# A two-layer graph network on one core: the prelude's order, the decoding of neighbour lists, and where the last lists are made

## The chip, the cores and the metric

The kernel runs on 1 core of a Trainium2 chip. The time is device microseconds of one execution; the number compared is the median over repeated executions. TensorE is called PE (PEld its weight loads), VectorE DVE, ScalarE ACT, GpSimd POOL, SyncE SP. Each engine works through its own instructions in the order of the program; DMA transfers are issued from the queues of SP, ACT and POOL.

## What is computed

x has 3327 rows of 512, adj is a symmetric 0/1 matrix of 3327 x 3327 with a full diagonal and some 9 ones in a row. Two layers, each with a residual and a normalisation:

```python
# layer 0: four heads of 128
feats = einsum('nf,hfo->hno', X, W)
e_s, e_n = feats . a_self, feats . a_neigh               # one number per head and node
logits = leaky_relu(e_s[:, :, None] + e_n[:, None, :], 0.2) + NEG_INF * (1 - A)
out = relu(concat_h(softmax(logits) @ feats) + b)
x = layernorm(x + out)
# layer 1
attn_a = sigmoid([adj @ x, x] @ Wa.T + ba);  attn_b = sigmoid([adj @ x, x] @ Wb.T + bb)
h = x @ W_sa;  scores = (h @ a_sa_left)[:, None] + (h @ a_sa_right)[None, :]
e = where(adj != 0, exp(-leaky_relu(scores, 0.01)), 0);  x_a = e / (sum(e) + 1e-5) @ h
x_b = adj @ (x @ W_gcnb) + b_gcnb
x = layernorm(x + sigmoid(attn_a * x_a + attn_b * x_b))
```

## The kernel before

**Sparse work.** The kernel reads adj once, makes a list of neighbours for each node, and then gathers rows by those lists. The 3328 padded nodes are 26 tiles of 128: a first group of 12 tiles and a second of 14 (`NG`). Within a group nodes are sorted by degree, so that tile j needs only `CAPS[j]` neighbour slots (14 down to 5, and 14 down to 4). Only if a check at the end finds something that the lists don't cover does `dense_pass` run; it doesn't with these inputs.

**Prelude (L199 to L634).** adj and x come in seven chunks of 512 columns (the last has 256). SP's queue holds the loads in this order: W0, x0, x1, then for each chunk 13 pairs of adjacency tiles (L221, `AT` = 12 buffers) and x of the chunk after next (L212, 3 buffers). ACT's queue loads the two rows a_neigh and a_self, W_sa and the two halves of a_sa. For each tile `features` (L362) makes 8 accumulations x W0 on PE (260 columns per half: 256 features and 4 score columns), ACT copies them into a row of 520, and POOL writes it to `table0` in DRAM (L379). The score columns of W0 are made first: DVE and POOL multiply W0 with a broadcast row, DVE reduces (L302, L309). The vectors of W_sa, needed for the scores of layer 1, are made by POOL products and DVE reductions (L339, L340).

**Lists.** For a chunk, `make_codes` (L389) multiplies the adjacency tiles with powers of two on PE, so that each block of 16 nodes becomes one number: a code of 16 bits and the block's number in its low bits. `turn_codes` transposes them. `top_codes` (L421) takes the 24 largest codes of each node (`S` = 24) with MAX8 and MATCH_REPLACE8 on 224 columns. `decode` (L427) splits off the highest bit of each code `LEVELS` = 4 times, giving 4 x 24 candidates, and `pick` (L445) takes the 24 largest of these 96 and turns them into node numbers, in `st0` or `st1`, and degrees. All of it is DVE work. `rank_a` and `rank_b` (L474, L484) rank a group's nodes by degree, with two matmuls and a scan. The first group's lists are sorted through DRAM: 12 indirect writes on POOL (L145), one load back (L529), then 12 gathers of x (`own_x`, L557); the tasks are handed out three at a time between projections (`later`). The second group's lists are sorted on PE, two of 14 steps in each of seven rounds of layer 0 (`sort1`, L534).

**The loop of the prelude (L608 to L634).** Three projections, then for each chunk: codes, one projection, turn, top, decode, pick, four projections. Ranks of the first group are ready in chunk 3's round, those of the second after chunk 6. Only then is layer 0 reached.

**Layer 0 (L863 to L922).** `gather` (L644) issues one indirect DMA on POOL for each slot of a tile (L667), into 7 buffers of up to 6 slots (`GB`, `U`), three tiles ahead. All gathers read `table0`, and so stand behind all its row writes. For a tile, `weigh_a` and `weigh_b` make the softmax weights on DVE; `attend` (L800) scales two of three gathered rows on DVE and one on ACT, and PE adds them up with an identity matrix (L820). Then come the residual (L898), the statistics, and the products with the score vectors `v1` (`columns1` to `columns3`, L834 to L848); groups of finished tiles are normalised and written to `table1`. The order of tiles (`order0`) begins with the first group's tiles 11, 10, 0, 1, 2 and so on: slots 6, 7, 16, 13, 12, 11. Tile 0 of each group has extra slots (`stair`), placed with `to_nodes` and `to_rows` on PE; `climb` prepares them.

**Layer 1 (L927 to L1122)** gathers from `table1` in the same manner and ends with the output's indirect writes.

Of the kernel before, what the change touches and what calls it, by code (L numbers as in the profile page):

```python
# [14 lines left out]
P = 128  # L15
# [14 lines left out]
LW = 32  # L30
# [4 lines left out]
AT = 12  # L35
# [44 lines left out]
def sparse_pass(  # L80
# [50 lines left out]
    B = len(STAIRS)  # L131
    C0 = CAPS[0]
# [6 lines left out]
    table1 = dram.tile([NP, ROW], F32, name="table1")  # L139
    own1 = dram.tile([NG[1] * P, 2, ROW], F32, name="own1")  # L140
    lists0 = dram.tile([NG[0] * P, LW], I32, name="lists0")

# [20 lines left out]
    ovf = const.tile([P, NT, 3], F32, name="ovf")  # L163
# [44 lines left out]
    def load_x(i):  # L208
        if i < len(chunks):
            cw = min(CH, NP - chunks[i])  # L210
            xc = xcs[i] = pj.tile([P, KT, CH], F32, tag="xc", name=f"xc{i}", bufs=3)
            nc.sync.dma_start(xc[:, :, :cw], xB[i] if cw == CH else xL)  # L212

    halves = halves_of(NT)
    loaded = {}

    def load_adj(i):
        cw = min(CH, NP - chunks[i])
        for q, (a, b) in enumerate(pairs_of(NT)):
# [7 lines left out]
    wsa0 = pj.tile([P, KT, F], F32, name="wsa0")  # L227
    nc.scalar.dma_start(wsa0, W_sa.rearrange("(k p) o -> p k o", p=P))
    asa_rows = []
    for s in range(2):  # L230
        a_row = pj.tile([P, F], F32, name=f"asa_row{s}")
        nc.scalar.dma_start(a_row, row_bcast(a_sa, F, s * F))
        asa_rows.append(a_row)
    load_x(1)
    for i in range(len(chunks)):
        load_adj(i)
        load_x(i + 2)
# [36 lines left out]
    all1 = p0.tile([P, ND * NM], F32, name="all1")  # L274
    nc.gpsimd.memset(all1, 1.0)

    st0 = p0.tile([P, NG[0], LW], I32, name="st0")
# [3 lines left out]
    count = dict(channel_multiplier=1, allow_small_or_imprecise_dtypes=True)  # L281
    W1 = S + 2 + H
# [11 lines left out]
    def st(t):  # L294
        return (st0[:, t, :], st0[:, t, S + 2 : S + 2 + H].bitcast(F32)) if t < NG[0] else (
            st1[:, t - NG[0], :], st1[:, t - NG[0], S + 2 : S + 2 + H]
        )

    for s in range(2):
        for hh in range(2):  # L300
            prod = pj.tile([P, KT, 2, FO], F32, tag="prod", name=f"prod{s}_{hh}", bufs=4)
            (nc.vector, nc.gpsimd)[s].tensor_mul(  # L302
                prod,
                w0[:, :, hh, 0 : 2 * FO].rearrange("p k (h o) -> p k h o", h=2),
                a_rows[s][:, hh * 2 * FO : (hh + 1) * 2 * FO]
                .rearrange("p (k h o) -> p k h o", k=1, h=2)
                .to_broadcast([P, KT, 2, FO]),
            )
            nc.vector.tensor_reduce(w0[:, :, s, 2 * FO + 2 * hh : 2 * FO + 2 * hh + 2], prod, AX.X, ALU.add)  # L309
# [12 lines left out]
    with nc.allow_non_contiguous_dma(reason="four vectors of 512, onto partitions"):  # L322
        for i, w in enumerate((Wa, Wb)):
            for s in range(2):
                src = w[0:1, s * F : (s + 1) * F].rearrange("o (k p) -> p (o k)", p=P)
                nc.gpsimd.dma_start(v1[:, :, 3 * s + 1 + i], src)
    nc.gpsimd.dma_start(bias0, row_bcast(b0, F))
# [5 lines left out]

    for s in range(2):
        for k in range(KT):
            prod = pj.tile([P, F], F32, tag="prod1", name=f"sprod{s}_{k}", bufs=2)
            nc.gpsimd.tensor_mul(prod, wsa0[:, k], asa_rows[s])  # L339
            nc.vector.tensor_reduce(v1[:, k, 3 - 3 * s : 4 - 3 * s], prod, AX.X, ALU.add)  # L340

    nc.gpsimd.tensor_add(v1[:, :, 4:6], v1[:, :, 4:6], v1[:, :, 1:3])
    nc.gpsimd.tensor_add(v1[:, :, 6], v1[:, :, 0], v1[:, :, 3])

    in_step = p0.tile([P, P], F32, name="in_step")
    nc.gpsimd.memset(in_step, 1.0)
    nc.gpsimd.memset(no_step, 0.0)
    for b, n in enumerate(STAIRS):
        o = sum(STAIRS[:b])
        nc.gpsimd.tensor_copy(to_row[:, o : o + n], ident[:, :n])  # L350
        nc.gpsimd.affine_select(
            in_step[:, o : o + n], in_step[:, o : o + n], pattern=[[0, n]], compare_op=ALU.is_equal, fill=0.0,
            base=-b, channel_multiplier=1,
        )
        nc.gpsimd.affine_select(
            no_step[:, b : b + 1], no_step[:, b : b + 1], pattern=[[0, 1]], compare_op=ALU.is_ge, fill=-BIG,
            base=n - 1, channel_multiplier=-1,
        )
# [3 lines left out]
    def features(t):  # L362
# [4 lines left out]
        pf = psf.tile([P, 2, 512], F32, tag="pf", name=f"pf{t}")  # L367
        for k, hh in ((k, hh) for hh in range(2) for k in range(KT)):
            nc.tensor.matmul(  # L369
                pf[:, hh, :HC], xc[:, k, o : o + P], w0[:, k, hh, :], start=(k == 0), stop=(k == KT - 1)  # L370
            )
        row = pj.tile([P, ROW], F32, tag="row", name=f"row{t}", bufs=4)
# [5 lines left out]
        nc.scalar.copy(st(t)[1], pf[:, 1, F // 2 : HC])  # L378
        nc.gpsimd.dma_start(table0[t * P : (t + 1) * P, :], row)  # L379

    widths = [32 * ((len(ms) + 3) // 4) for ms in halves]
    vs, pvs, ents, cands, codes_left = {}, {}, {}, {}, {}
# [6 lines left out]
    def make_codes(i):  # L389

        own0, nt = span(i)[:2]
        v = vs[i] = p0.tile([P, 2, CH], F32, tag="v", name=f"v{i}", bufs=2)
        for half, ms in enumerate(halves):
# [1181 lines left out]
```

## Time and profile before

| | |
|---|---|
| 14 runs | median 959.32 us (953.42 to 963.75) |
| profiled execution | 965.76 us, its span 963.8 us |
| prelude up to the first tile's weights | 0 to 219.5 us |
| layer 0 | 219.5 to some 556 us |
| layer 1 | some 556 to 963.8 us |
| busy: PE, DVE, POOL, ACT | 798.4, 742.3, 615.7, 278.7 us |
| granted TensorE clock, mean | 0.898 |
| DMA: bytes, mean rate | 221.41 MB, 230 GB/s |

Busy time of POOL counts the issue of a gather at about 1.0 us; the next one starts 0.3 us later even when nothing holds it, so POOL can be saturated at three quarters busy. A busy time of PE counts matmuls that overlap. The rate of DMA counts both the prelude's loads and everything that is written.

### The profile page before, as it was taken

How to read it: one execution, taken by the hardware profiler on the slowest of the kernel's cores; microseconds unless marked ns; L12 is line 12 of the kernel's file. 1: busy time of each engine (PE TensorE's matmuls, PEld its weight loads, DVE VectorE, ACT ScalarE, POOL GpSimd, SP SyncE). 2: the span in 40 equal slices, each digit the busy share in tenths (PEclk: the TensorE clock that was granted, in tenths of full speed). 3: DMA queues.
4: the chain of work that ended last, by engine and by line, in shares of the span. 5: the costliest groups of instructions: out<-in, count | busy, mean ns of one | idle time of the engine just before them, and what ended most of it. 6: DMA issues, size and time to landing. Idle time of an engine off the chain costs nothing.

```text
span 963.8 us, 10097 instructions
## 1 busy us (share of the span) xinstructions
PE 798.4 (83%) x2516; PEld 419.7 (44%) x2516; DVE 742.3 (77%) x2175; ACT 278.7 (29%) x820; POOL 615.7 (64%) x654
## 2 busy tenths in 40 slices
PE   4398997328999887979969839998999989899893
PEld 3176775114545444434434414444434434344341
DVE  4277677786988588687757838799989989989873
ACT  1022121002435244335333403213222232232241
POOL 6611134775677767677777467777777777777511
PEclk9699998557899899899988958999989999999998
DMA  9799899998678777887777266767676676666401
GB/s 319 285 356 401 339 339 372 379 400 287 171 207 248 208 243 222 270 271 232 229 224 232 105 177 190 197 187 186 192 192 197 184 192 190 187 187 182 139 22 47
DMA packets 71986, 221.41 MB, mean 230 GB/s; under 512 B 12912, under 2 KB 16960, under 8 KB 71024
## 3 DMA queue, kind: packets, MB, share of 16 engines
q0 software_dynamic: 46560, 153.64, 53.9%
q1 hardware_dynamic: 22704, 64.94, 17.7%
q10 hardware_dynamic: 2656, 2.10, 0.7%
q8 instruction: 23, 0.38, 0.2%
q14 instruction: 43, 0.35, 0.1%
HBM read 199.78 MB, written 28.32 MB: 237 GB/s over the span
## 4 chain that ended last, share of the span: by engine, by line
PE 42%; DVE 20%; DMA 15%; POOL 12%; issue 7%; ACT 3%; DVEq 0%; POOLq 0%; ACTq 0%
PE acc L820 17%; DMA g<-table,srt 10%; PE pf L369 9%; POOL g L667 9%; DVE sw L1025 7%; PE po L1065 5%; PE acc L1046 4%; DMA at<-in_adjB 4%; DVE g L1027 3%; PE pcol L844 2%; DMA a_row<-in_a_self 1%; POOL sprod L339 1%; PE sorted L548 1%; ACT za L1110 1%; DVE za L1093 1%
## 5 line engine op out<-in xcount | busy, mean ns | idle before, releaser
L667 POOL DMA_INDIRECT g<-table,srt x464 | 482.4, 1040 | 160.6 <-issue 119.5
L820 PE MATMUL acc<-g,ident 128*128 128x512 f32 x504 | 241.6, 637 | 3.2 <-DVE g L814 1.6
L1025 DVE SCALAR_TENSOR_TENSOR sw<-g,e,sw 128x512 f32<-128x512 f32 x226 | 169.4, 749 | 12.8 <-ACT sw L1009 8.5
L820 PEld LDWEIGHTS acc<-g,ident 128*128 128x128 f32 x504 | 101.4, 206 | 126.5 <-issue 90.1
L1046 PE MATMUL acc<-g,ident 128*128 128x512 f32 x262 | 128.6, 618 | 24.9 <-DVE g L1027 15.1
L369 PE MATMUL pf<-w,xc 128*128 128x260 f32 x416 | 102.7, 409 | 13.8 <-DVE w L309 13.8
L814 DVE TENSOR_TENSOR g<-g,w 128x512 f32<-128x512 f32 x176 | 112.4, 696 | 0.6
L1065 PE MATMUL po<-wg,sT 128*128 128x512 f32 x208 | 98.1, 616 | 0.0
L369 PEld LDWEIGHTS pf<-w,xc 128*128 128x128 f32 x416 | 84.2, 205 | 29.8 <-DVE w L309 14.2
L1065 PE MATMUL po<-wsa,sT 128*128 128x512 f32 x208 | 95.2, 601 | 0.3 <-ACT sT L1058 0.3
L812 ACT ACTIVATE g<-g,w 128x128 f32<-128x128 f32 x304 | 91.6, 390 | 0.7 <-DVE w L795 0.7
L1046 PEld LDWEIGHTS acc<-g,ident 128*128 128x128 f32 x262 | 49.1, 193 | 95.8 <-issue 43.7
L379 POOL DMA_DIRECT2D table<-row x26 | 14.4, 554 | 87.3 <-ACT st L378 87.3
L1027 DVE TENSOR_TENSOR g<-g 128x512 f32<-128x512 f32 x95 | 65.7, 691 | 3.3
L1095 ACT ACTIVATE za<-za 128x512 f32<-128x512 f32 x26 | 16.4, 631 | 170.7 <-DVE za L1093 170.7
L1065 PEld LDWEIGHTS po<-wg,sT 128*128 128x128 f32 x208 | 41.3, 200 | 52.4 <-issue 52.1
L1065 PEld LDWEIGHTS po<-wsa,sT 128*128 128x128 f32 x208 | 40.2, 194 | 51.4 <-issue 49.1
L145 POOL DMA_INDIRECT out<-za,srt x26 | 28.6, 1099 | 50.0 <-ACT za L1110 43.9
L397 PE MATMUL pc<-at,pow 128*32 128x512 bf16 (+1 forms) x182 | 24.0, 433 | 36.3 <-DMA at<-in_adjB 22.4
L844 PE MATMUL pcol<-v,xt 128*128 128x8 f32 x208 | 30.6, 274 | 27.9 <-ACT xt L841 27.9
L782 ACT ACTIVATE w<-w 128x40 f32<-128x40 f32 (+10 forms) x26 | 6.2, 237 | 149.7 <-DVE w L781 149.7
L844 PEld LDWEIGHTS pcol<-v,xt 128*128 128x128 f32 x208 | 29.3, 215 | 34.5 <-ACT xt L841 33.4
(252 smaller groups left out, 932.4 us busy)
## 6 DMA issues: line engine op xcount, KB each, us to landing
at<-in_adjB SPq DMA_DIRECT2D x78, 512.0 KB, 11.6
g<-table,srt POOLq DMA_INDIRECT x464, 3.8
table<-row POOLq DMA_DIRECT2D x26, 260.0 KB, 6.0
xc<-in_xB SPq DMA_DIRECT2D x6, 1024.0 KB, 7.2
own<-in_xo SPq DMA_DIRECT2D x1, 3640.0 KB, 31.9
own<-table SPq DMA_DIRECT2D x1, 3640.0 KB, 47.0
at<-in_adjL SPq DMA_DIRECT2D x13, 256.0 KB, 13.2
table<-x1a SPq DMA_DIRECT2D x12, 260.0 KB, 4.6
```

Of the source, the lines that this page charges most:

```text
L145: put = nc.gpsimd.indirect_dma_start(out=dst, out_offset=bass.IndirectOffsetOnAxis(ap=rows, axis=0), in_=src, in_offset=None, bounds_check ...
L369: nc.tensor.matmul(pf[:, hh, :HC], xc[:, k, o : o + P], w0[:, k, hh, :], start=(k == 0), stop=(k == KT - 1))
L397: nc.tensor.matmul(pc[32 * c : 32 * c + 32, : nt * P], pow2[:, s, :], loaded[i, m], start=(s == 0), stop=(m + 1 not in ms or s == 3),)
L667: nc.gpsimd.indirect_dma_start(out=buf[:, q - q0, :], out_offset=None, in_=table[:, :], in_offset=bass.IndirectOffsetOnAxis(ap=srt[g][:, i ...
L812: nc.scalar.activation(gv[:, h, :], gv[:, h, :], AF.Copy, scale=w[:, s, h : h + 1])
L814: nc.vector.tensor_tensor(gv, gv, w[:, s, :].rearrange("p (h o) -> p h o", o=1).to_broadcast([P, H, FO]), ALU.mult)
L820: nc.tensor.matmul(acc, ident, row, start=(lean and s == 0), stop=(s == CAPS[j] and j not in T0))
L844: nc.tensor.matmul(pcol, xt1[:, k, :], v1[:, k, :], start=(k == 0), stop=(k == KT - 1))
L1025: nc.vector.scalar_tensor_tensor(sw, g[:, i, 0:F], e[:, s : s + 1], sw, ALU.mult, ALU.add)
L1027: nc.vector.tensor_add(g[:, i, 0:F], g[:, i - 1, 0:F], g[:, i, 0:F])
L1046: nc.tensor.matmul(plain[j], to, row, start=(not sums_of_two and i == 0), stop=(sums_of_two and i == len(rows) - 1),)
L1065: nc.tensor.matmul(proj[j], sT[:, k, :], wt[:, k, :], start=(half + k == 0), stop=(half + k == KT))
```

## The change

The diff touches the prelude and the first rounds of layer 0.

- **Loads.** SP's order becomes W0, x0 (in two pieces), then for each chunk 8 pairs of adjacency tiles, x of the next chunk, 5 pairs. `AT` goes from 12 to 11. W_sa comes last, in two pieces into adjacency buffers; a_sa comes word by word on POOL's queue, partition by partition.
- **W0's score columns** are 32 DVE instructions that multiply and sum 128 columns each. The first two tiles are projected without them (`feature_sums` with 256 columns), and their scores are added after (`score_sums`).
- **Rows** go to `table0` from ACT's queue. The rank word goes from POOL's.
- **Order.** `make_codes` takes a chunk in parts (4, 4, 3 and 2 pairs), and projections stand between the parts, in an order written out by hand.
- **Decoding.** The highest bit of all 24 codes is split off once. Of what remains the 8 largest numbers are taken, and three more bits are split off these. `pick` takes 24 of 48 candidates. For chunks 0 to 2 part of it runs on POOL (`finish(nc.gpsimd, ...)`).
- **W_sa's vectors** are made on PE in layer 0: four rounds of four transposes, a copy by ACT, and four matmuls (`scores_vectors`).
- **Lists inside layer 0.** Codes of chunk 5 are made before layer 0; its lists, chunk 6, the second group's ranks and all 14 steps of its sort are made in the first three rounds (`lists`). Six of the 12 `own_x` stand before the first gathers, six behind the third tile's.
- **PSUM.** The list pools live on until round 3, so the pools of layer 0 have one buffer each until then and two after. Two tiles of layer 1 change their pool.

```diff
-AT = 12
+AT = 11
+PARTS = ((0, 4), (4, 8), (8, 11), (11, 13))
...
-    wsa0 = pj.tile([P, KT, F], F32, name="wsa0")
-    nc.scalar.dma_start(wsa0, W_sa.rearrange("(k p) o -> p k o", p=P))
...
     for i in range(len(chunks)):
-        load_adj(i)
-        load_x(i + 2)
+        load_adj(i, 0, 1)
+        load_x(i + 1)
+        load_adj(i, 2, 3)
+    wsa0 = []
+    for k in range(0, KT, 2):
+        wsa0 += [p0.tile([P, 2, CH], F32, tag="at", name=f"wsa0_{k}", bufs=AT)]
+        nc.sync.dma_start(wsa0[-1], W_sa[k * P : (k + 2) * P, :].rearrange("(k p) o -> p k o", p=P))
...
     for s in range(2):
-        for hh in range(2):
-            prod = pj.tile([P, KT, 2, FO], F32, tag="prod", name=f"prod{s}_{hh}", bufs=4)
-            (nc.vector, nc.gpsimd)[s].tensor_mul(prod, ...)
-            nc.vector.tensor_reduce(w0[:, :, s, 2 * FO + 2 * hh : 2 * FO + 2 * hh + 2], prod, AX.X, ALU.add)
+        for k, h in ((k, h) for k in range(KT) for h in range(H)):
+            hh, col = h // 2, 2 * FO + h
+            prod = pj.tile([P, FO], F32, tag="prod", name=f"prod{s}_{k}_{h}", bufs=2)
+            nc.vector.tensor_tensor_reduce(
+                prod, w0[:, k, hh, h % 2 * FO : (h % 2 + 1) * FO], a_rows[s][:, h * FO : (h + 1) * FO],
+                1.0, 0.0, ALU.mult, ALU.add, w0[:, k, s, col : col + 1],
+            )
...
+    def scores_vectors():
+        sums = psl.tile([P, CH], F32, tag="pc1", name="asa_sums")[:, : 2 * KT].rearrange("p (k s) -> p k s", s=2)
+        for k in range(KT):
+            pt = psl.tile([P, CH], F32, tag="pc0", name=f"wsa_t{k}").rearrange("p (o w) -> p o w", o=KT)
+            for o in range(KT):
+                nc.tensor.transpose(pt[:, o, :], wsa0[k // 2][:, k % 2, o * P : (o + 1) * P], ident)
+            turned_ = p0.tile([P, KT, P], F32, tag="v", name=f"wsaT{k}", bufs=2)
+            nc.scalar.copy(turned_, pt)
+            for o in range(KT):
+                nc.tensor.matmul(sums[:, k, :], turned_[:, o, :], asa[:, o, :], start=(o == 0), stop=(o == KT - 1))
+        nc.vector.tensor_copy(v1[:, :, 0], sums[:, :, 1])
+        nc.vector.tensor_copy(v1[:, :, 3], sums[:, :, 0])
+        nc.vector.tensor_add(v1[:, :, 4:6], v1[:, :, 4:6], v1[:, :, 1:3])
+        nc.vector.tensor_add(v1[:, :, 6], v1[:, :, 0], v1[:, :, 3])
...
-        nc.gpsimd.dma_start(table0[t * P : (t + 1) * P, :], row)
+        nc.scalar.dma_start(table0[t * P : (t + 1) * P, :], row)
...
+    def decode(eng, i):
...
+        ids, code = apart(ent, S, 0)
+        bit = first_bit(ids, code, S, 0)
+        rest = kept("rest", i, [S])
+        nc.vector.tensor_sub(rest[:, :nt], ent, bit)
+        most = kept("most", i, [8])
+        for j in range(nt):
+            nc.vector.max(most[:, j, :], rest[:, j, :])
+        ids, code = apart(most[:, :nt], 8, 1)
+        for at in range(S, S + 8 * (LEVELS - 1), 8):
+            bit = first_bit(ids, code, 8, at)
+            nc.vector.tensor_sub(code[:, :nt], code[:, :nt], bit[:, :nt])
...
+    feature_sums(0)
+    feature_sums(1)
+    for t in range(2):
+        score_sums(t)
+        feature_rows(t)
+    more(2)
+    make_codes(0, 0, 1)
+    more(1)
+    make_codes(0, 2, 3)
+    turn_codes(0)
+    top_codes(0)
+    finish(nc.gpsimd, 0)
+    more(2)
     stairs_ready()
+    more(1)
+    make_codes(1, 0)
+    more(1)
+    make_codes(1, 1, 2)
+    more(1)
+    make_codes(1, 3)
+    turn_codes(1)
+    top_codes(1)
+    finish(nc.gpsimd, 1)
+    more(2)
+    for part in range(3):
+        make_codes(2, part)
+        more(1)
+    make_codes(2, 3)
+    turn_codes(2)
+    top_codes(2)
+    finish(nc.gpsimd, 2, 0)
+    more(4)
+    make_codes(3, 0, 1)
+    more(1)
+    sort0(*rank_b(0))
+    make_codes(3, 2, 3)
+    turn_codes(3)
+    top_codes(3)
+    finish(nc.vector, 3)
+    more(2)
...
+    finish(nc.vector, 4)
+    more(NT)
+    climb(0, p0, psl.tile([P, CH], F32, tag="pc0", name="climb0")[:, : B + H])
+    make_codes(5)
+    turn_codes(5)
...
+    def lists(i):
+        if i == 0:
+            make_codes(6)
+            top_codes(5)
+            turn_codes(6)
+            finish(nc.vector, 5)
+        if i == 1:
+            scores_vectors()
+            psum = small("pv1sum")[:, :NCOL]
+            for k in range(KT):
+                nc.tensor.matmul(psum, ones, v1[:, k, :], start=(k == 0), stop=(k == KT - 1))
+            nc.vector.tensor_copy(v1sum, psum)
+            top_codes(6)
+            finish(nc.vector, 6, 1)
+        if i == 2:
+            sort1(rank_b(1))
...
-        if 0 < i <= 7:
-            sort1(rankis[1], 2 * i - 2, 2 * i)
-        if i == 8:
+        lists(i)
+        if i == 4:
             climb(1, m0, ...)
```

`lists(i)` stands in round i behind `attend` and the sums of the tile before, and ahead of the next tile's `weigh_a`.

## The prediction

> **What bounds the kernel now.** I first read the page's chain of waits (PE 42%, DVE 20%, DMA 15%, POOL 12% of the span): no engine leads, so I took it by stages. The busy times by stretches (columns: PE, PEld, DVE, ACT, POOL busy with instruction counts, granted clock, DMA share, GB/s):
>
> ```profile
> 36.00:40.00 4.00, 0.31 (x2) 0.31 (x2) 0.00 (x0) 0.00 (x0) 3.94 (x29) 0.50 0.23 93
> 112.00:117.00 5.00, 5.00 (x27) 4.02 (x26) 4.55 (x24) 0.83 (x5) 0.54 (x1) 1.00 0.54 215
> 243.00:311.00 68.00, 68.00 (x197) 33.75 (x197) 61.01 (x157) 28.77 (x96) 49.37 (x49) 0.97 0.73 209
> 311.00:343.00 32.00, 26.40 (x83) 14.08 (x82) 16.72 (x59) 10.53 (x36) 24.51 (x25) 0.89 0.75 208
> ```
>
> The prelude (0 to 199 us) is supply: DMA moves 405 to 417 GB/s when it is fed, and it starves at 36-40, where PE waits for POOL's constants (L589), and where PE runs four projections in a row (64 matmuls of L369, 14.06 us) and frees no adjacency buffer (L221 waits for L397). In layer 0 the shares mislead: PE is full from 243 to 311, but POOL is full in another sense. Its timeline, instruction by instruction (start, duration, line, then idle before it):
>
> ```profile
> 180.45 0.95 POOL L667 DMA_INDIRECT g<-table,srt  x1 [0.31 <-issue]
> ...
> 230.33 0.95 POOL L667 DMA_INDIRECT g<-table,srt  x1 [6.22 <-PE acc L820]
> ...
> 252.18 1.14 POOL L667 DMA_INDIRECT g<-table,srt  x1 [3.81 <-PE acc L820]
> ...
> 530.03 0.95 POOL L667 DMA_INDIRECT g<-table,srt  x1 [0.30 <-DMA g<-own,srt]
> ```
>
> From 180.45 to 531.0 there are 258 issues (254 gathers, 4 scatters) and 18.5 us of idle time (6.2, 3.8, then 3.5, 3.1, 1.8): 332 / 258 = 1.287 us an issue, so POOL never rests otherwise. The chain agrees: from 322 it runs through gathers, not through PE. Layer 0 ends some 25 us after POOL's last gather. So I follow **T**, the end of that last gather (531.0). The DVE timeline says what held the first tiles back:
>
> ```profile
> 199.33 0.39 DVE L72 MAX8 ent<-pv 128x8 f32<-128x224 f32 x1
> ...
> 211.80 0.52 DVE L478 TENSOR_TENSOR oh<-degs,deg 128x350 f32<-128x350 f32 x1
> ...
> 219.53 0.18 DVE L769 TENSOR_TENSOR w<-g,srt 128x24 f32<-128x24 f32 x1 [0.53 <-DMA g<-table,srt]
> ```
>
> Chunk 6's lists and the second group's ranks end at 219; then the first tile is weighed, although POOL has gathered since 180 and stands on full buffers at 224.
>
> **Part 1, the supply.** Terms: an adjacency pair 512 KB, a chunk of x 1024 KB, a table row 260 KB (the DMA issues) at 410 GB/s: 1.28, 2.56, 0.65 us. A projection costs PE 3.51, 26 code matmuls about 2.3 (17 took 1.33 at 117), the turn 1. W0, x0 and the two rows are in by 8.5 (a_row landed at 10.9 with 2.5 MB more ahead of it). PE projects two tiles by 15.6 and meets the DVE's 32 products of w0. No such operation is in the trace: below it lies the 128x128 DVE row (L542, 0.25-0.28), above it the 128x512 reduction (L340, 0.69), so 8 to 22 us in place of the eight instructions of 1.22; I take 0.35, nearer the width, 11 us, ending at 20. [...] At 22 us it would still move nothing: PE then starts chunk 0's codes at 36 rather than 29, and the DMA fills its eleven buffers by 31.
>
> Then PE alternates. Walking both queues with these terms, chunks 0 to 4 are turned at 36, 58, 85, 114 and 140 (before: 52, 75, 102, 127.5, 154). PE still waits: tile 16 for x4, which now lands behind eight pairs (9 us), tile 20 for x5 (8), tile 24 for x6 (5); behind each wait stand code matmuls that would free buffers, so SP halts 5 and 3 us with eleven full. The last projection ends at 152; ACT's copies take 1.2, the row's landing 6.0 (the L379 rows), so gathers may start at **G = 160** (before 180.45). Rows leave POOL's queue for ACT's: 26 issues of 0.4-0.5 there, beside 5.4 us of ACT work per 25, each right behind the copies that it sends, so it delays nobody. POOL gets 15 small operations a chunk for chunks 0 to 2 and two word-wise loads of a_sa (0.8 each, as L326); 0.2 us (128x8) to 1.23 (128x512) each, I take 0.4; DVE waits in `pick` for them, about 1 us, and saves 2. That has 4 us of slack before tile 19's projection, behind which rank_b's matmuls stand; without the cover, the excess shifts chunk 3. The rank word goes to POOL, 12 scatters (15.4), the load of lists0 (8) and six own_x (7.7) end near 150, ahead of G. climb's matmul waits on PE for the end of chunk 4 on DVE (160); chunk 5's codes are queued behind it, so the eleven buffers stand full from 149 to 162. What is left then (5.5 MB: chunk 5's last pairs, chunk 6, W_sa) shares the DMA with gathers (0.27 MB per 1.287 us, 207 GB/s): in by 190, ahead of its use in layer 0. own1's two loads follow it on SP and are wanted at 355 (first L661). Bounds of G: all bytes to x6 with the rows, 53 MB, at 410 GB/s give 131, plus 2 at the start, two projections and the landing: 148; from above 175, when every one of the three waits doubles.
>
> **Part 2, the decoding.** MAX8 takes 0.395 at 224 columns and 0.261 at 96: 1.05 ns a column, so 48 columns save 0.05 on each of 20: 1.0 us. The decode before is 3.6 us for 15 operations (163.3 to 166.9); now 22 narrower ones, 4.6. Sum zero: a chunk stays at 20.5 us, chunk 6 at 12.5. W_sa's eight POOL products (9.8) leave a queue that now has room.
>
> **Part 3, the lists in layer 0.** This is the term that decides. The first tile is weighed at A = G + six gathers (7.7) + landing (3.8, 6.3 under load) = 172. From there DVE's queue in order, with rows of before: weigh and scale the first tile 4.3 (219.5 to 223.9); chunk 5 20.5; second tile 5.0; sum and statistics 1.6; then `scores_vectors`. Its copies wait for PE, which does the second tile's sums first (until A+35), then four rounds of transposes, ACT copy and matmuls: L837 to L844 took 1.33, plus 1.06, so 9.6 and 2 more for v1sum's round trip: DVE is free at A+48. Behind this wait stand chunk 6 (12.5), rank_a (0.5), the third tile's weights (4.1): A+65. The third tile has 16 rows: PE needs 18 us (242.5 to 260.3), and rank_b's matmuls stand behind them: A+86. rank_b 4.9, fourteen sort rows of 0.76 (L542 to L544 spacing) 10.7, last matmul and copies 1.7, weights 2.2: the fourth tile is scaled from A+105; its first buffer is free at **R** = A+110 = 282. Before, that was 267. [...]
>
> POOL meanwhile can fill seven buffers ahead: the first three tiles (29 gathers) and 36 more are issued by G + 71 x 1.287 = 251 (six own_x now among them); then it waits for R. T = R + (258-65) x 1.287 + idle later. Of the 8.4 us of idle after 263 I keep half: T = 282 + 248.4 + 4 = 534.4, **3.4 us later than before**. The ten sort rows that leave tiles 3 to 7 (DVE 7.6, PE 7) shorten engines that wait for POOL there: nothing. PE would need about 250 us from its fourth tile (290 less 33 idle and 7), so PE stays ahead of T. Layer 1 is unchanged but for two bank names.
>
> The profiled execution took 965.76 (span 963.8), the median is 959.32: I carry the difference over, 959.3 + 3.4 = **963**.
>
> **Rivals.** *The head start survives (not slower).* If DVE's chain in the first three tiles is short, POOL decides: T = G + (258+6) x 1.287 + idle. It turns at R = 278.6, a chain of 106.6 from A. For it: 16.8 of the 110 are DVE waiting for scores, 10 waiting for PE behind the third tile, on an engine that is otherwise idle. Against: both waits follow from program order. With both hidden R = 255 and T = 507; with half of them R = 268.5, T = 520.9, 10 us earlier than before: 949. *The supply doesn't come earlier.* SP has eleven buffers, not twelve, and every x chunk but the first two lands between halves. With the waits doubled G = 175, R = 297: T = 549, 978. For it: PE idles near 22 us in my walk already. Against: the 15 us before 41 are won in any case. *Nothing to see:* gains and losses cancel, 959.
>
> **Chances.** Forecast (953 to 971) 0.5, head start 0.28, late supply 0.22. A measurement of this kernel tells 0.3%, 2.9 us. Faster: most of the head start and a tenth from the forecast, 0.34; same 0.16, from the forecast; slower 0.50. The range, 944 to 978, takes in the head start down to R = 264 and the late supply up to its own number; it leaves out some 2 in 10. The forecast's own is 953 to 971.
>
> **What would show it.** G: the first L667-type gather near 160. The chain: three stretches in the first 110 us in which PE idles and DVE works on lists, with DVE waiting for PE before the copies of v1 and of the ranks. POOL: one wait of 16 and one of 15 us before the fourth tile's buffers. Wrong would be a fourth tile that starts on PE before 270, or a POOL that idles after it for more than 10 us, or a first gather after 170.

## The result, and the profile after

| | before | changed | 
|---|---|---|
| median | 959.35 us | 1000.72 us (10 runs, 994.1 to 1009.25) |
| ratio, 95% interval | | 1.0423 (1.0401 to 1.0445) |
| profiled execution, span | 963.8 us | 999.4 us |
| mean granted TensorE clock | 0.898 | 0.896 |
| first gather of layer 0 | 180.45 us | 182.43 us |
| end of its last gather (T) | 531.0 us | 571.1 us |

The kernel became 41 us slower; 963 was predicted, in a range that ended at 978. T moved by 40.1, so nearly everything was lost before T. What follows T takes no longer than before (999.4 - 571.1 = 428 us, 963.8 - 531.0 = 433).

The busy times of four stretches of the changed kernel (columns as in the first fence of the prediction: PE, PEld, DVE, ACT, POOL, granted clock, DMA share, GB/s):

```profile
122.00:136.00 14.00, 0.88 (x6) 0.68 (x5) 12.80 (x52) 0.00 (x0) 9.91 (x11) 0.62 1.03 377
229.00:243.00 14.00, 10.84 (x58) 8.16 (x56) 0.21 (x3) 2.34 (x4) 10.65 (x12) 0.83 1.04 414
260.00:283.00 23.00, 20.36 (x52) 10.53 (x52) 10.40 (x24) 7.12 (x26) 7.46 (x8) 0.81 0.27 72
316.00:571.00 255.00, 221.38 (x662) 112.24 (x661) 187.36 (x560) 105.76 (x343) 188.74 (x193) 0.94 0.78 236
```

The first is a hole in PE inside the prelude. The second is one in DVE, early in layer 0. In the third POOL works 7.5 of 23 us and the DMA is down to 27%; before, POOL was never that empty between 243 and 343. The fourth is the steady state, which is what it was (193 issues in 255 us). The timelines say what stands behind these holes. PE in the prelude (start, duration, line, then the idle time before and what ended it):

```profile
80.34 5.81 PE L380 MATMUL pf<-w,xc 128*128 128x260 f32 x16 [4.67 <-DMA xc<-in_xB]
...
102.91 10.76 PE L380 MATMUL pf<-w,xc 128*128 128x260 f32 x48 [2.20 <-DMA xc<-in_xB]
...
135.49 9.06 PE L380 MATMUL pf<-w,xc 128*128 128x260 f32 x32 [13.12 <-DMA xc<-in_xB]
...
169.01 9.36 PE L380 MATMUL pf<-w,xc 128*128 128x260 f32 x32 [13.33 <-DMA xc<-in_xL]
```

These are the projections of tiles 12, 16 to 18, 20 and 21, and 24 and 25. SP's queue shows why x is late:

```profile
93.80 27.98 SPq L228 DMA_DIRECT2D at<-in_adjB  x13
122.68 0.33 SPq L217 DMA_DIRECT2D xc<-in_xB  x1
126.36 31.49 SPq L228 DMA_DIRECT2D at<-in_adjB  x13
157.90 0.56 SPq L217 DMA_DIRECT2D xc<-in_xL  x1
```

x5 is issued at 122.68, behind five pairs of chunk 3 and eight of chunk 4, for which SP needed 28 us because the buffers were full: in the first 200 us it waited 60.2 us in all for PE's code matmuls. PE can start on x5 12.8 us after its issue, with the DMA full (a share of 1.03 and 377 GB/s from 122 to 136). PE's program, however, wants tile 20 ahead of chunk 4's codes, which free those buffers. So PE, SP and the buffers hand the wait round: no codes until x is there, no x until pairs are out, no free buffer until there are codes. The last piece, x's last chunk, goes round in the same way.

POOL's timeline has the consequences in layer 0, and DVE's has the waits behind them:

```profile
182.43 0.94 POOL L766 DMA_INDIRECT g<-table,srt  x1 [29.57 <-DMA table<-row]
...
273.41 0.94 POOL L766 DMA_INDIRECT g<-table,srt  x1 [23.67 <-PE acc L918]
...
315.87 0.94 POOL L766 DMA_INDIRECT g<-table,srt  x1 [20.34 <-ACT srt L885]
```

```profile
195.72 0.18 DVE L868 TENSOR_TENSOR w<-g,srt 128x24 f32<-128x24 f32 x1 [16.56 <-DMA at<-in_adjL]
...
242.79 0.17 DVE L362 COPY v<-asa_sums 128x4 f32<-128x4 f32 x1 [16.14 <-PE asa_sums L361]
...
282.79 0.52 DVE L561 COPY tots<-tot 128x350 f32<-128x350 f32 x1 [11.21 <-PE tot L559]
```

The rows land at 182, and POOL has stood idle for 30 us by then. The first tile is weighed at 195.72. (The releaser named there, an adjacency transfer, is not what that line reads.) DVE waits 16 us for W_sa's sums and 11 for the ranks' matmuls, and POOL, with its seven buffers full, waits 23.7 and 20.3 us, where before it waited 6.2 and 3.8.

T can be counted as a sum: T = first gather + issues x the time of one + POOL's waits of over 1 us. In the traces of the table below an issue takes 1.26 to 1.29 us. Changed kernel: 182.4 + 264 x 1.275 + 52.2 = 571.1. Before: 180.45 + 258 x 1.287 + 18.5 = 531.0. The 40.1 us are thus 2.0 of first gather, 4.4 of issues and 33.7 of waits. This counts where the time went and does not say why. The experiments are read by the same three terms.

### The profile page after: what moved, and what is told of

The parts are those of the page before. It is cut to its first block, busy times and chain, and to the rows that moved or that the text cites. A ratio compares the mean times of both kernels' runs of the same rounds, so it can differ in the third digit from the quotient of the medians.

```text
span 999.4 us, 10380 instructions
## 1 busy us (share of the span) xinstructions
PE 811.9 (81%) x2596; PEld 430.8 (43%) x2596; DVE 730.6 (73%) x2253; ACT 280.8 (28%) x824; POOL 595.5 (60%) x663
## 3 DMA queue, kind: packets, MB, share of 16 engines
q0 software_dynamic: 44592, 146.73, 49.7%
## 4 chain that ended last, share of the span: by engine, by line
PE 34%; DMA 21%; DVE 17%; POOL 12%; issue 11%; ACT 4%; SPq 0%; DVEq 0%; POOLq 0%; ACTq 0%
PE acc L918 16%; POOL g L766 11%; DMA g<-table,srt 10%; PE pf L380 7%; DVE sw L1142 6%; DMA xc<-in_xB 4%; DMA at<-in_adjB 3%; PE acc L1163 2%; PE po L1182 2%; PE pcol L942 2%; DVE g L1144 2%; DMA table<-row 2%; POOL out L147 1%; ACT za L1227 1%; DMA xc<-in_xL 1%
## 5 line engine op out<-in xcount | busy, mean ns | idle before, releaser
L766 POOL DMA_INDIRECT g<-table,srt x464 | 476.2, 1026 | 224.1 <-issue 123.8
L918 PE MATMUL acc<-g,ident 128*128 128x512 f32 x504 | 240.5, 635 | 17.0 <-DVE g L912 16.3
L1142 DVE SCALAR_TENSOR_TENSOR sw<-g,e,sw 128x512 f32<-128x512 f32 x226 | 169.4, 750 | 12.4 <-ACT sw L1126 8.2
L380 PE MATMUL pf<-w,xc 128*128 128x260 f32 (+1 forms) x416 | 106.8, 418 | 44.8 <-DMA xc<-in_xB 31.4
L1163 PEld LDWEIGHTS acc<-g,ident 128*128 128x128 f32 x262 | 49.7, 195 | 94.1 <-issue 44.8
L147 POOL DMA_INDIRECT out<-za,srt x26 | 28.6, 1101 | 49.7 <-ACT za L1227 43.6
L396 ACT COPY row<-pf 128x512 f32<-128x512 f32 x26 | 15.3, 587 | 142.7 <-PE pf L380 118.4
L73 DVE MAX8 ent<-pv 128x8 f32<-128x224 f32 x26 | 10.0, 384 | 56.6 <-PE pv L448 56.6
L942 PEld LDWEIGHTS pcol<-v,xt 128*128 128x128 f32 x208 | 30.0, 222 | 41.9 <-ACT xt L939 41.4
```

The source lines that it names most:

```text
L147: put = nc.gpsimd.indirect_dma_start(out=dst, out_offset=bass.IndirectOffsetOnAxis(ap=rows, axis=0), in_=src, in_offset=None, bounds_check ...
L380: nc.tensor.matmul(pf[:, hh, :w], xc[:, k, o : o + P], w0[:, k, hh, :w], start=(k == 0), stop=(k == KT - 1))
L766: nc.gpsimd.indirect_dma_start(out=buf[:, q - q0, :], out_offset=None, in_=table[:, :], in_offset=bass.IndirectOffsetOnAxis(ap=srt[g][:, i ...
L918: nc.tensor.matmul(acc, ident, row, start=(lean and s == 0), stop=(s == CAPS[j] and j not in T0))
L942: nc.tensor.matmul(pcol, xt1[:, k, :], v1[:, k, :], start=(k == 0), stop=(k == KT - 1))
L1142: nc.vector.scalar_tensor_tensor(sw, g[:, i, 0:F], e[:, s : s + 1], sw, ALU.mult, ALU.add)
```

## The experiments

One chip ran the kernels that fell on it 14 to 17% slower, the kernel before 15% (1105 and 1103 us in its two visits). The seven runs that fell on it are told at the end and are not compared with the others; six of those kernels were run again.

| run | first gather | first tile weighed | POOL's waits | T | median us | ratio to before, interval |
|---|---|---|---|---|---|---|
| before | 180.5 | 219.5 | 18.5 | 531.0 | 959.35 | |
| changed | 182.4 | 195.7 | 52.2 | 571.1 | 1000.72 | 1.0423 (1.0401-1.0445) |
| x earlier | 161.9 | 176.2 | 52.8 | 550.6 | 981.21 | 1.0209 (1.0191-1.0228) |
| W_sa's sums after chunk 6 | 182.0 | 196.2 | 42.9 | 559.9 | 991.64 | 1.0335 (1.0306-1.0365) |
| own rows ahead | 183.4 | 196.3 | 63.7 | 576.5 | 1007.03 | 1.0468 (1.0440-1.0497) |
| lists ahead | 181.9 | 242.4 | 45.5 | 564.4 | 994.83 | 1.0354 (1.0330-1.0378) |
| x and sums | 156.0 | 171.3 | 43.5 | 534.4 | 967.83 | 1.0087 (1.0059-1.0115) |
| and sort spread, 2 buffers | 161.2 | 176.5 | 58.8 | 553.3 | 980.85 | 1.0200 (1.0157-1.0242) |
| and sort spread, 3 buffers | 157.1 | 172.2 | 33.3 | 528.8 | 961.64 | 1.0018 (0.9991-1.0044) |
| x earlier, all lists ahead | 161.8 | 215.8 | 28.8 | 527.6 | 949.37 | 0.9881 (0.9844-0.9917) |
| the same, own rows ahead | 163.3 | 223.3 | 41.9 | 535.1 | 960.03 | 0.9980 (0.9958-1.0002) |
| the same, own rows last | 153.7 | 204.9 | 11.9 | 511.0 | 946.59 | 0.9860 (0.9835-0.9884) |
| and DVE's order shortened | 158.7 | 206.3 | 10.5 | 516.1 | 947.96 | 0.9854 (0.9827-0.9882) |

The profile columns are of one execution each; the medians are of several. Executions differ: four kernels (x earlier, x and sums, and the sort spread on 2 and on 3 buffers) have the same instructions ahead of the first gather, and in their traces it came at 161.9, 156.0, 161.2 and 157.1. Three traces are of executions away from their median: "x earlier, all lists ahead" 960.2 us (the other four took 949.0 to 950.5), the same with own rows ahead 966.1 (median 960.0), own rows last 942.5 (median 946.6). Times read from these three are therefore up to some 10 us off.

**x half a chunk earlier.**

```diff
     for i in range(len(chunks)):
         load_adj(i, 0, 1)
-        load_x(i + 1)
+        if i == 0:
+            load_x(1)
         load_adj(i, 2, 3)
+        load_x(i + 2)
```

> Each chunk of x from the third on is loaded half a chunk earlier: ahead of the eight adjacency pairs it stood behind. Theory (x stands behind eight pairs on SP, and these wait for buffers that PE frees only behind the projections that wait for x): the waits of 13.1 and 13.3 us before tiles 20 and 24 fall under 3 us each, the first gather moves from 182.4 to 156-166, the last gather from 571 to 545-555, the time from 1001 to 975-985. Rival (eleven buffers or the DMA rate hold the prelude back, whatever the order of x): the first gather stays within 5 us of 182 and the time within 5 of 1001. Rival (only the lists inside layer 0 count): the first gather is earlier, but the last gather and the time stay within 5 us of the changed kernel's.

981.2. Nothing else differs, not the bytes, not the buffers. SP's and PE's rows for the same x5, and POOL's first gather:

```profile
107.09 1.51 SPq L217 DMA_DIRECT2D xc<-in_xB  x1
...
133.34 0.89 SPq L217 DMA_DIRECT2D xc<-in_xL  x1
```

```profile
117.10 9.80 PE L382 MATMUL pf<-w,xc 128*128 128x260 f32 x32 [1.06 <-DMA xc<-in_xB]
...
143.52 10.24 PE L382 MATMUL pf<-w,xc 128*128 128x260 f32 x32 [0.90 <-DMA xc<-in_xL]
```

```profile
161.88 0.94 POOL L768 DMA_INDIRECT g<-table,srt  x1 [11.71 <-DMA at<-in_adjB]
...
253.54 0.94 POOL L768 DMA_INDIRECT g<-table,srt  x1 [23.82 <-PE acc L920]
...
295.79 0.94 POOL L768 DMA_INDIRECT g<-table,srt  x1 [20.19 <-ACT srt L887]
```

The waits before tiles 20 and 24 go from 13.1 and 13.3 to 1.1 and 0.9 us, SP's 13 pairs ahead of each of these two chunks of x take 20.1 and 23.8 us instead of 28.0 and 31.5, and the first gather comes 20.5 us earlier, as do T and, to 1 us, the time. POOL's two waits keep their lengths (23.8, 20.2): they belong to the chain that starts at the first tile, which moves as a whole. Both rivals fall: eleven buffers and the DMA's rate allow a first gather at 162, and the lists alone don't explain the loss.

**W_sa's vectors behind chunk 6's lists.** The next edits were made to the changed kernel, each alone.

```diff
         if i == 1:
+            top_codes(6)
+            finish(nc.vector, 6, 1)
             scores_vectors()
...
-            top_codes(6)
-            finish(nc.vector, 6, 1)
```

> In the second tile's round, chunk 6's lists stand ahead of W_sa's vectors on VectorE. Theory (the list chain of the first three tiles decides when the fourth tile's buffers come free): the 16.1 us in which VectorE waits for the sums are filled by 12.5 us of lists, the fourth tile starts 10-14 us earlier, and the time is 987-992. Rival (supply alone explains the 41 us): no change, within 4 us of 1001. Rival (the chain is as long, the wait only moves behind the third tile): the wait for the rank matmuls, 11.2 us before, becomes over 20 us, and the time stays within 4 us of 1001.

991.6, a gain of 9. DVE and POOL:

```profile
243.24 0.17 DVE L362 COPY v<-asa_sums 128x4 f32<-128x4 f32 x1 [2.22 <-PE asa_sums L361]
...
271.33 0.52 DVE L561 COPY tots<-tot 128x350 f32<-128x350 f32 x1 [11.89 <-PE tot L559]
```

```profile
261.96 0.95 POOL L766 DMA_INDIRECT g<-table,srt  x1 [12.15 <-PE acc L918]
...
304.74 0.94 POOL L766 DMA_INDIRECT g<-table,srt  x1 [20.94 <-ACT srt L885]
```

The copies start at 243 as they did, but the wait is now filled: 16.1 became 2.2. The wait for the ranks stays (11.9), and POOL's first wait shrinks by 11.5. So the chain decides, and the wait did not just move to the next one.

**All own rows ahead of the first gather.**

```diff
-    for j in order0[:6]:
+    for j in order0[: NG[0]]:
         own_x(j)
     for i in range(AHEAD):
         got[order0[i]] = gather(table0, order0[i])
-    for j in order0[6 : NG[0]]:
-        own_x(j)
```

> All twelve fetches of own rows stand ahead of the first gather (six stood behind the third tile's). Theory: POOL waits 23.7 and 20.3 us for buffers behind them, so 7.7 us fewer issues there only lengthen these waits: the sum of both becomes 50-54 us, and the time stays within 3 us of 1001. Rival (layer 0 is as long as POOL's issues, idle or not): 993.

1007.0: no gain, as expected, but some 4 us worse by the ratios, outside the 3 us of the theory; the two intervals just touch. POOL's first two waits are 33.6 and 21.3, 54.9 together (50 to 54 were expected). They took up the 7.7 us and 3 more: VectorE's waits for W_sa's sums and for the ranks are 18.1 and 12.3 instead of 16.1 and 11.2. x's last chunk found PE waiting 17.2 us instead of 13.3, and the first gather came 1 us later. What the place of these fetches costs is followed up below.

**The lists ahead of the first tile's weights.**

```diff
+    ready = [[], []]
+    make_codes(6)
+    top_codes(5)
+    turn_codes(6)
+    finish(nc.vector, 5)
+    top_codes(6)
+    finish(nc.vector, 6, 1)
+    to1 = rank_b(1)
+    sort1(to1)
     weigh_a(order0[0])
     weigh_b(order0[0])
-    ready = [[], []]
```

`lists` then keeps only `scores_vectors` and its total, in round 1.

> The lists of chunks 5 and 6, the ranks and the sort of the second group go ahead of the first tile's weights, as far as VectorE's order goes; W_sa's vectors stay in the second tile's round. Theory (in layer 0 these lists cost their own time and in addition 16.1, 11.2 and about 5 us in which VectorE waits for PE between them): the first tile is weighed at 240-250 instead of 196, but the fourth tile starts only some 55-65 us after that instead of 112, that is 10-20 us earlier than now, and the time is 981-991. Rival (the lists are partly hidden inside layer 0, and ahead of it they are not): the fourth tile later by 10 us or more, the time 1010-1035.

994.8: better, by less than expected. The first tile is weighed at 242.4, inside the bounds, and the wait for W_sa's sums is still there:

```profile
270.03 0.17 DVE L362 COPY v<-asa_sums 128x4 f32<-128x4 f32 x1 [16.89 <-PE asa_sums L361]
```

```profile
250.64 1.17 POOL L766 DMA_INDIRECT g<-table,srt  x1 [18.56 <-PE acc L918]
...
288.89 1.20 POOL L766 DMA_INDIRECT g<-table,srt  x1 [20.80 <-PE acc L918]
```

POOL's waits add up to 45.5 instead of 52.2, and T is 6.8 earlier. The theory forgot that POOL's buffers are full after some 39 issues, at 232: with the first tile this late it waits for that tile's buffers, and then a second time, behind the tile whose scaling waits for DVE to get W_sa's sums. So lists ahead of layer 0 win little by themselves; they need the earlier supply too.

**Both of the first two edits.**

> The same kernel on another chip (on the one before, the kernel before itself took 1105 us). Both edits together: x half a chunk earlier (alone 19.5 us below the changed kernel) and chunk 6's lists ahead of W_sa's vectors (alone 9). Theory (the first gather and the chain from the first weighed tile to the fourth tile's buffers add up): 968-974. Rival (they hide each other, the later of the two decides): 978-983.

967.8: a little more than the sum (1000.7 - 19.5 - 9.1 = 972.1); the first gather of this trace, on another chip, came 6 us earlier than with x earlier alone. They add up; neither hides the other.

**The sort spread over rounds 3 to 7**, on top of those two, three of its fourteen rows a round (the second group's `climb` moves from round 4 to 8, behind it):

```diff
         if i == 2:
-            sort1(rank_b(1))
+            to1.append(rank_b(1))
+        if 3 <= i < 8:
+            sort1(to1[0], 3 * i - 9, 3 * i - 6)
```

> The same kernel again. As the run with both, and the sort of the second group is spread: three of its fourteen rows in each of rounds 3 to 7, in a PSUM bank of its own, instead of all of them ahead of the fourth tile's weights. Theory (the sort's 15 us of matmuls and the 5 us before them stand between the third tile and the fourth's buffers, and later engines wait for POOL): POOL's last wait before the fourth tile's buffers, 20 us, falls under 8, and the time is 952-960. Rival (spread rows cost as much in the rounds they go to): within 4 us of the run with both.

980.9, 13 us slower than without: theory and rival both miss. POOL's long wait is gone as expected, but there are new ones in every round (33 us between 300 and 375). DVE shows where they come from:

```profile
278.00 0.28 DVE L604 TENSOR_SCALAR row_is<-columns,to 128x128 f32<-128x128 f32 x1 [7.41 <-PE sorted L610]
...
297.02 0.29 DVE L604 TENSOR_SCALAR row_is<-columns,to 128x128 f32<-128x128 f32 x1 [4.67 <-PE sorted L610]
...
313.94 0.29 DVE L604 TENSOR_SCALAR row_is<-columns,to 128x128 f32<-128x128 f32 x1 [5.27 <-PE sorted L610]
```

A round's third row needs an operand buffer that PE frees with its matmul for the first row, and that matmul stands behind a whole tile's sums. There are two such buffers. In the kernel before, two rows went to a round and fitted.

```diff
-            row_is = ls.tile([P, P], F32, tag="row_is", name=f"row_is{t}", bufs=2)
+            row_is = lsx.tile([P, P], F32, tag="row_is", name=f"row_is{t}", bufs=3)
...
-            spread = ls.tile([P, n, W1], F32, tag="spread", name=f"spread{t}", bufs=2)
+            spread = lsx.tile([P, n, W1], F32, tag="spread", name=f"spread{t}", bufs=3)
```

> The same kernel again (the chip before ran the kernel before in 1103 us). As the run with the sort spread over rounds 3 to 7, which took 981 instead of the 952-960 expected, but with three buffers each for the sort's two operands instead of two. Theory (the sort itself belongs in those rounds; three rows a round on two buffers make VectorE wait each round until PE, behind a whole tile's sums, has read the first row: 7.4, 4.7 and 5.3 us in the trace): these waits vanish, POOL's waits in rounds 3 to 8 fall from 35 us to under 15, the time is 950-962. Rival (the rows cost these rounds as much wherever they wait): 975-985.

961.6, as the theory had it; PE now takes a round's three rows in one go (six matmuls in 2.28 us at 270.00, 283.75, 296.64 and 308.67), and POOL's waits from 290 on fall from 38.8 to 16.6 us. So the third buffer is worth some 18 us (1.0200 against 1.0018), and the spread sort some 6 (1.0018 against 1.0087). The run is level with the kernel before.

**x earlier, and all lists ahead.** Chunk 5's codes stand ahead of `climb` on PE; chunks 5 and 6, W_sa's vectors and the ranks stand ahead of the first tile's weights, and the sort goes two rows a round from round 1. With the lists gone from the rounds, layer 0 has its second PSUM buffers from the start, so that this run does not tell the two apart:

```diff
-    climb(0, p0, psl.tile([P, CH], F32, tag="pc0", name="climb0")[:, : B + H])
     make_codes(5)
     turn_codes(5)
+    climb(0, p0, psl.tile([P, CH], F32, tag="pc0", name="climb0")[:, : B + H])
...
+    finish(nc.vector, 6, 1)
+    scores_vectors()
...
+    to1 = rank_b(1)
     weigh_a(order0[0])
...
+        if 0 < i <= 7:
+            sort1(to1, 2 * i - 2, 2 * i)
```

> The same kernel again. x half a chunk earlier, chunk 5's codes ahead of the stairs' matmul on PE, the lists of chunks 5 and 6, W_sa's vectors and the ranks all ahead of the first tile's weights, the sort two rows a round as in the kernel before. Theory (with the first gather near 162 and nothing of the lists between the first tiles, POOL stays fed): the first tile is weighed at 195-210, POOL's idle time in layer 0 is under 20 us, the last gather ends at 510-522, the time is 938-952, faster than the kernel before. Rival (lists ahead of layer 0 delay the first tile past POOL's seven full buffers, as in the run with the lists ahead alone): POOL's idle time stays over 40 us and the time is 965-980.

949.4, faster than before by 1.2% and inside the theory's range. In its trace the first tile came later than expected (215.8), and POOL's waits are 28.8 us, between the two theories; but this is the execution that took 960.2 us, 11 more than the others, so these two figures are not those of the median. The longest wait, 15.6, ends with the first tile's sums. The own rows were then moved both ways, to the front and behind the third tile's gathers:

> The same kernel again. As the run before it, and all twelve fetches of own rows stand ahead of the first gather. Theory (POOL now has few waits left, so the 7.7 us of six issues count, unlike in the changed kernel): 4-8 us faster than the run before it. Rival (they only lengthen waits, or the fetches delay the last loads of the prelude): no gain, or up to 4 us slower.

> The same kernel again. As the run with the lists ahead (949), but all twelve fetches of own rows stand behind the third tile's gathers, none ahead of the first. Theory (twelve ahead cost 11 us because 3 MB of fetches push back the last adjacency loads and with them the first tile's weights; behind the third tile POOL waits for buffers anyway): the six that go behind make the first tile 2-5 us earlier and the time 942-948. Rival (the fetches' place counts only by POOL's issues): within 2 us of 949.

960.0 and 946.6. Six fetches (1.5 MB) ahead of the gathers instead of behind cost 10.7 us, and taking away the other six brings 2.8 (that much the intervals do not separate). PE's and POOL's rows, first with all of them ahead, then with none:

```profile
145.13 7.79 PE L382 MATMUL pf<-w,xc 128*128 128x260 f32 x32
...
174.73 0.50 PE L661 MATMUL climb<-of,to_row 128*128 128x14 f32 x2
```

```profile
148.17 1.01 POOL L619 DMA_INDIRECT x1a<-in_x,srt  x1 [7.28 <-DMA srt<-lists]
...
234.48 0.94 POOL L773 DMA_INDIRECT g<-table,srt  x1 [28.81 <-PE acc L925]
```

```profile
137.19 8.80 PE L382 MATMUL pf<-w,xc 128*128 128x260 f32 x32
...
159.50 0.50 PE L661 MATMUL climb<-of,to_row 128*128 128x14 f32 x2
```

```profile
153.70 1.00 POOL L773 DMA_INDIRECT g<-table,srt  x1 [18.38 <-DMA at<-in_adjB]
...
215.48 0.94 POOL L773 DMA_INDIRECT g<-table,srt  x1 [3.32 <-PE acc L925]
```

The `climb` stands behind chunk 5's codes on PE, so its start tells when that chunk's last pair had landed: 174.7 against 159.5. The first tile follows (223.3, 204.9), then POOL's wait (28.8, 3.3). The fetches leave from an idle queue (POOL had waited 7.3 us ahead of the first), but with their 12 x 256 KB under way the last adjacency pairs land more slowly: PE's code matmuls, each waiting for a pair, start 2.4 to 2.9 us apart (154.17 to 172.64) against 1.3 to 1.7 (147.16 to 157.42). Not all of the 15 us between the two rows of `climb` are theirs: PE began the last two projections 7.9 us later in the first trace (145.1 against 137.2) and ended them 6.9 later (152.9 against 146.0), and the first fetch left at 148.2. From the end of these projections to `climb` it is 21.8 and 13.5 us. The 8.3 us between these, in one execution each, agree with an estimate: at 410 GB/s, within the 405 to 417 that the DMA moved in the prelude of the kernel before, 3.1 MB take 7.7 us.

**DVE's order shortened**, on top of the last. `climb`'s small steps go behind chunk 5's lists, the copies of W_sa's sums behind the first tile's weights. The third tile's gathers and all own rows stand behind `climb` and go with it:

```diff
     finish(nc.vector, 5)
+    climb(0, p0, psl.tile([P, CH], F32, tag="pc0", name="climb0")[:, : B + H])
...
+    sums1 = scores_vectors()
     to1 = rank_b(1)
     weigh_a(order0[0])
     weigh_b(order0[0])
+    scores_copies(sums1)
```

> As the run with the own rows last, and VectorE's order shortened up to the first tile's weights: the stairs' small steps behind chunk 5's lists (VectorE waited 5.7 us for them), the copies of W_sa's sums behind the first tile's weights (PE's part stays ahead of the ranks), their total in round 1 (2.3 and 2.1 us). Theory (the first tile's weights are what POOL's first wait in layer 0, 15.6 us, hangs on): first tile at 203-209 instead of 216, that wait under 8 us, the time 934-944. Rival (the last chunk's loads, not VectorE, hold the lists there): first tile less than 3 us earlier than with the own rows last, time within 3 us of it.

948.0: nothing more, as the rival had it. The first tile came at 206.3, no earlier than in the run that it builds on (204.9), and the first gather at 158.7 instead of 153.7. The wait of 15.6 us that the theory set out from belongs to the long execution of the run with six fetches ahead. By then POOL waits 11 us in all of layer 0, so there is little left for DVE's order to win.

**On the slower chip.** Ratios to the kernel before, taken on that chip, for five of the seven runs (the sort on two buffers, 1113.8 us, and the own rows ahead, 1107.3, have none): x and sums 0.9997 (0.9875-1.0120), all lists ahead 1.0111 (1.0024-1.0197), three buffers 1.0133 (1.0064-1.0202), own rows last 1.0022 (0.9966-1.0079), and a first form of the shortened order 0.9950 (0.9908-0.9992), in which PE's part of W_sa's vectors stood behind the ranks:

> As the run with the own rows last, and VectorE's order shortened up to the first tile's weights: the stairs' small steps go behind chunk 5's lists (VectorE waited 5.7 us for them), the copies of W_sa's sums behind the ranks and their total into round 1 (2.3 and 2.1 us). Theory (the first tile's weights are what POOL's first wait in layer 0, 15.6 us, hangs on): first tile 8-12 us earlier than in the run with the lists ahead, that wait under 6 us, the time 934-944. Rival (the chunks' loads, not VectorE, hold the lists there): first tile less than 3 us earlier, time within 3 us of the run with the own rows last.

There it failed: 1101.7, the first tile at 244.6 as with the own rows last on that chip, and DVE waited 15.9 us for the sums, because on PE they now stood behind rank matmuls that wait for DVE. The form above keeps PE's part ahead. On this chip the version with all lists ahead is 1.1% slower than the kernel before, where on the other it was 1.2% faster, and the gain of the best version is not found.

## Why the prediction was wrong

**The step that failed is G**, the first gather: "gathers may start at **G = 160**", got from "tile 16 for x4, which now lands behind eight pairs (9 us), tile 20 for x5 (8), tile 24 for x6 (5)". G was 182.4, 22.4 us late. The mechanism was named rightly, x behind eight pairs, with codes behind the waiting projections. Its size was not, and neither was the rest of the walk. The last projection was to end at 152 and ended at 178.4:

- 12.2 us are the waits for x: 2.2, 13.1 and 13.3, with 4.7 and 0.9 for x3 and x2, which I had as none, 34.2 us instead of 22.
- 6.2 us are the projections of tiles 12, 20 and 24, which took 5.8, 5.6 and 5.9 us at a granted clock of 0.64 to 0.67, where others take 3.7 at 1.00. I priced each at 3.51, from four in a row. In the trace before five of the 26 already took 5.1 to 6.4 us.
- 5.4 us were lost ahead of all this: chunk 0 was turned at 41.4 instead of 36. x0 was there at 10.5 instead of 8.5, and two of the first three projections took 6.5 and 6.4 us.
- 2.6 us are spread over the rest, and 4 came back, since the first gather left 4.1 us after the last projection instead of 8.

I reckoned each wait by itself, from when x was issued, and let the queue recover between. In the trace the lag grows: chunks 0 to 4 were turned at 41, 66, 95, 121 and 154, that is 5, 8, 10, 7 and 14 us late. That one chunk's lag delays the buffers which the next x waits for follows from the order of the two programs; it was not tried by itself. My rival "the supply doesn't come earlier" doubled the waits, went to G = 175 and 978 us, and stopped short of it.

With x half a chunk earlier G was 161.9. That this is close to 160 is luck. The 160 contain 22 us of waits for x, and that run has 2.0. Without these waits 138 is left of my walk, 24 us less than was measured, and less even than the 148 that I had worked out from the bytes alone. In that run PE waited 8.9 us for adjacency tiles (2.0 in the changed kernel), the projections of tiles 20 and 21 took 9.8 us together and those of 24 and 25 10.2, where tiles 22 and 23 took 3.8 each, though hardly a wait for x stood before them (1.1 and 0.9 us), and the first gather left 8.1 us after the last projection. So the place of x costs the changed kernel 20.5 us of G, which the edit shows; but the walk was too short in its other parts as well, above all in the projections and the waits for adjacency tiles.

**The chain from the first tile was nearly right.** From the first weighed tile, DVE was to reach chunk 6's lists at A + 48 (measured 49.7), the ranks at A + 86 (87.1), after a wait of 16.8 for W_sa's sums (16.1) and one of 10 for the ranks (11.2). Chunks 5 and 6 were to take 20.5 and 12.5 us and took 20.1 and 12.8. Two terms were short. The fourteen sort rows with their last matmul and copies took 16.3 us instead of 12.4: I used the spacing of rows that ran two at a time, and fourteen in a row on two buffers alternate between DVE and PE, with 0.3 to 1.1 us of waiting on DVE ahead of seven of them. From scaling the fourth tile to POOL's next issue it was 9.7 us, not 5. The remaining 1.6 are 1.1 at the ranks and rounding. So R was A + 120 instead of A + 110: 195.7 + 120.2 = 315.9, against 282.

**The sum.** R was 33.9 us late: 22.4 from G, 1.3 from G to A, 10.2 from the chain. After R, 2.9 more (waits of 8.2 instead of 4, less 1.3 in the issues). That makes 36.8, and 963 + 36.8 = 999.8, against 1000.7. POOL's two waits, 23.7 and 20.3 where 16 and 15 were written, are the same chain seen from the other side.

**What held.** T decides and POOL sets it; layer 1 was unchanged. The list chain, the part on which the forecast of a loss rested, is real: filling its largest wait brought 9 us, and the sort 6 to 7 more. What was written to show the prediction wrong did so: a first gather after 170. W0's 32 products were given 0.35 us each, 11 in all; they took 6.9 (7.65 to 14.57), one every 0.21, less even than the 8 to 22 us between which two rows of the trace before had set them. It moved nothing, as stated. The head start, a rival at 0.28, existed only in the DVE's first weights (195.7 against 219.5 before), and the chain used it up.

**Not tried:** the narrower decoding, the rows on ACT's queue and POOL's earlier constants were not undone one by one. The best version contains all three, so they do not cost what was lost; what each is worth is open.

## What to carry over

When a kernel interleaves two streams through one in-order queue and one pool of buffers, write the consumer's order and the loader's order side by side and look for the first place where the consumer wants B before A and the loader brings A before B; here moving five loads half a chunk was worth 20 us. Walk both queues together through all chunks: here the lag grew from 5 to 14 us. And when a forecast term comes out right in a later run, see whether its parts did too: 160 and 161.9 agreed with 22 us of waits in the one and 2 in the other. And judge a step moved onto an idle engine by its buffers and its bytes too: three rows on two buffers cost 18 us, and 1.5 MB of fetches from an idle queue cost 11. The version that loads x earlier, makes all lists ahead and fetches its own rows last ran at 0.986 of the time before (946.6 us) on one chip, and at 1.0022 on the slower one.

## What had not been expected of the hardware

One chip ran the kernels that fell on it at 1.14 to 1.17 times the time, at a granted clock of 0.84 to 0.87 for the kernel before, where the other chips had 0.90 to 0.91. In the kernel with all lists ahead, between 174 and 215 us there, DVE's small instructions start 1.4 us apart; on another chip they ran without such gaps (DVE there: first tile at 215.8, here at 244.2):

```profile
187.43 0.21 DVE L473 CAST idsFalse<-ent 128x96 int32<-128x96 f32 x1 [1.02 <-issue]
188.83 0.21 DVE L474 TENSOR_SCALAR idsFalse<-idsFalse 128x96 int32<-128x96 int32 x1 [1.19 <-DVE idsFalse L473]
190.23 0.26 DVE L476 TENSOR_TENSOR codeFalse<-ent,idsFalse 128x96 f32<-128x96 f32 x1 [1.19 <-issue]
```

Each takes as long as on the other chip (0.21, 0.21, 0.26), but the time between these is ended by nothing outside DVE that the profile shows; other gaps of the stretch, of 1.7 to 3.2 us, it puts down to another core or an unknown queue. By the slices of the page DVE was busy 3 and 2 tenths of the time from 166 to 221 there and 8 and 6 tenths from 168 to 216 on the other chip, while the DMA moved as much in both (380 and 377 GB/s there, 378 and 392). The cause is open.
